# Twenty-five blocks of an adjacency matrix, transposed by a DMA from SBUF to SBUF instead of by TensorE and ScalarE

## The chip, the cores and the metric

The kernel runs on one core of a Trainium2 chip. A core has a matrix engine (TensorE, PE in the profile; its weight loads are PEld), a vector engine (VectorE, DVE), an activation engine (ScalarE, ACT), GpSimd (POOL), and SyncE (SP), which here only issues DMAs. The engines run side by side, each through its own instructions in order, and wait for one another through semaphores. DMAs are moved by 16 DMA engines that all issuers share. The metric is the device time of one execution in microseconds (us), lower being better.

## The reference

A graph of 3,125 nodes with 128 features and 100,000 edges (`src`, `dst`, one of eight types) passes through four graph layers, each followed by a residual and a layer norm. Cut to what matters here:

```
edge_index = stack([src, dst])
x = layernorm(x + L0(x, src, dst))              # three GCN layers: row = src, col = dst
x = layernorm(x + L1(x, edge_index))            # sum of x @ W.T + b over incoming edges
x = layernorm(x + L2(x, edge_index))            # GIN: (1 + eps) x + sum over incoming edges, batchnorms
x = layernorm(x + L3(x, edge_index, type))      # two relational layers: a mean for each of 8 types

# in L0
deg  = segment_sum(1, row)                      # with a self loop for each node
dinv = rsqrt(deg)
h    = segment_sum(dinv[row] * dinv[col] * (h @ W)[col], row) + b
```

L1 and L2 sum over the edges that enter a node, L0 over those that leave it. With the edges as a matrix of counts, L1 and L2 multiply by that matrix and L0 by its transpose. L0 also needs a degree for each node before its first product.

## The kernel before, in words

Nodes are padded to 3,200, that is 25 blocks (`NB`) of 128 (`P`). The kernel has two stretches: one that builds dense matrices of edge counts from the edge list and stores them in HBM, and one that multiplies by them.

**The build** takes the 25 blocks of destination nodes in turn. For block b, `total(b, behind)` counts the edges from each source block s into b:

- VectorE makes one-hot tiles by comparing keys with a ramp (`one_hot`, whose instruction is recorded on L191): `lo` and `hi` for each of two halves u of the block. For the first 15 blocks (`ND`) it also makes `rhq` (L191) and `rlo` (L331), which serve the counts by edge type.
- TensorE multiplies one-hots into the PSUM tile `bld`, which has two buffers. L356 makes the counts of all edges. L339, in `packed_counts`, makes the counts by type, for the first 15 blocks.
- ScalarE evicts `bld`: L359 into `at` (four times in a block), L342 into `rb` (sixteen times in each of the first 15 blocks).
- SP stores `rb` as eight DMAs of 400 KB into `rel` (L369), for the first 15 blocks.

The finished `at` of block b is a tile of 128 destinations by 25 blocks of 128 sources, bf16, 800 KB. `stored(b, at)` is called half-way through the next block's `total`. It adds the self loops on VectorE (L376), stores `at` to `adj_t` (L377), makes the transposed tile `av`, 128 x 3,200 (L378 to L383), stores that to `adj` (L384), and multiplies it by a vector of ones in seven matmuls (L388) that accumulate over the 25 blocks in two PSUM tiles `leave`: the degrees. `at` and `av` have two buffers each.

The transpose in `stored` is 25 TensorE transposes of 128 x 128 (L382), in groups of 13 and 12 into two of the `bld` tiles, each group evicted by one ScalarE copy (L383).

The loop over s also runs the search for the next blocks' edges: small VectorE instructions (L262 to L320) and indirect DMAs issued by GpSimd (L270, L290). These come once for two blocks.

A scheduler places the instructions of each engine in an order of its own, from the program's order and its own expectation of when things are ready. An engine keeps to the order that it was given. So where L388 stands in TensorE's order, and where L384 and L369 stand in SP's, is fixed before the kernel runs.

**After the build** the degrees are copied out of PSUM (L424 to L427), transposed, and turned into `dinv` (L430 to L438). Then the features are scaled and split in two (L662, L583, L584), and the first product begins.

**The products** of the first three layers load `adj` (`load`, L594); L1 and L2 load `adj_t` (L599). ScalarE and VectorE cast the loaded blocks to a wider type (L611, L613) and TensorE multiplies (L628). The relational layer after them reads `rel` (L757), casts (L767), and multiplies (L885). None of these lines is touched.

Of the kernel before, what the change touches and what calls it, by code (L numbers as in the profile page):

```python
# [9 lines left out]
BF = mybir.dt.bfloat16  # L10
# [11 lines left out]
P = 128  # L22
D = 128
N = 3125
NB = 25
# [20 lines left out]
def cols(m0, nb):  # L46
    return slice(m0 * P, (m0 + nb) * P)
# [26 lines left out]
def listed(ctx: ExitStack, tc: tile.TileContext, p: dict, out: bass.AP, bad):  # L74


    nc = tc.nc
# [6 lines left out]
    identb = const.tile([P, P], BF, name="identb")  # L84
# [81 lines left out]
    psum = lists.enter_context(tc.tile_pool(name="f_ps", bufs=1, space=PSUM))  # L166
    with tc.tile_pool(name="f_w", bufs=1) as wp, tc.tile_pool(name="f_bg", bufs=1) as bg:
# [28 lines left out]
        with tc.tile_pool(name="f_t1", bufs=1) as t1:  # L196
# [13 lines left out]
            with tc.high_priority():  # L210
# [5 lines left out]
                t = psum.tile([P, 512], F32, name="mi", tag="mi", bufs=2)  # L216
# [127 lines left out]
            def total(b, behind):  # L344
                at = t1.tile([P, NB, P], BF, name="at", bufs=2)
                rb = t1.tile([P, R * NB, 64], U16, name="rb", bufs=2) if b < ND else None
                for u in range(64 // PU):
                    lo = t1.tile([P, PU // 2, P, 2], BF, name="lo", bufs=2)
                    one_hot(lo, 0, b, u, P)
                    hi = t1.tile([P, PU // 2, 2 * NB, 2], BF, name="hi", bufs=2)  # L350
                    last[0] = one_hot(hi, 1, b, u, 2 * NB, iota50)
                    for v in range(PU // PA):
                        pt = psum.tile([P, PA, 64], F32, name="bld", tag="bld", bufs=2)
                        for k in range(PA):
                            j = v * PA + k
                            nc.tensor.matmul(pt[:, k, : 2 * NB], lo[:, j // 2, :, j % 2],  # L356
                                             hi[:, j // 2, :, j % 2], start=True, stop=True)
                        c0 = 2 * (u * PU + v * PA)
                        nc.scalar.copy(  # L359
                            at[:, :, c0 : c0 + 2 * PA].rearrange("p s (j h) -> p s j h", h=2),  # L360
                            pt[:, :, : 2 * NB].rearrange("p j (h s) -> p s j h", h=2),
                        )
                    if u == 0 and behind is not None:
                        stored(*behind)
                    if b < ND:
                        packed_counts(b, u, lo, rb)
                if b < ND:
                    for r in range(R):
                        nc.sync.dma_start(  # L369
                            rel[r][b].rearrange("p s d -> p (s d)").bitcast(U16),  # L370
                            rb[:, r * NB : (r + 1) * NB, :].rearrange("p s j -> p (s j)"),
                        )
                return b, at

            def stored(b, at):
                nc.vector.tensor_add(at[:, b, :], at[:, b, :], identb)  # L376
                nc.sync.dma_start(adj_t[b], at)  # L377
                av = t1.tile([P, NP], BF, name="av", bufs=2)  # L378
                for m0, nb in ((0, 13), (13, 12)):
                    t = psum.tile([P, 2048], BF, name="bld", tag="bld", bufs=2)  # L380
                    for k in range(nb):
                        nc.tensor.transpose(t[:, cols(k, 1)], at[:, m0 + k, :], identb)  # L382
                    nc.scalar.copy(av[:, cols(m0, nb)], t[:, : nb * P])  # L383
                nc.sync.dma_start(adj[b], av)  # L384
                for i in range(7):
                    w = min(512, NP - 512 * i)
                    q = 32 * (i % 4)
                    nc.tensor.matmul(leave[i // 4][q : q + 32, :w], onesb, av[:, 512 * i : 512 * i + w],  # L388
                                     start=(b == 0), stop=(b == NB - 1), skip_group_check=True)
# [14 lines left out]
            for s in range(SB):  # L404
# [8 lines left out]
                if 2 * s + 1 < NB:  # L413
                    built = total(2 * s + 1, built)
            stored(*built)

            tc.add_manual_dep(words.ins, started[0].ins.name, WAIT, reason="the search comes first")

            dinv = const.tile([P, NB], F32, name="dinv")
            for g in range(2):  # L420
                t = psum.tile([P, 512], F32, name="mi", tag="mi", bufs=2)
# [19 lines left out]
        psum = ctx.enter_context(tc.tile_pool(name="f_bk", bufs=1, space=PSUM, reuse_waits="tile"))  # L441

        def bank(tag):

            return psum.tile([P, 512], F32, name=tag, tag=tag, bufs=4 if tag == "x" else 2)
# [122 lines left out]
        with tc.tile_pool(name="f_nd", bufs=1, reuse_waits="tile") as nd:  # L568
# [85 lines left out]
            t = psum.tile([P, 512], F32, name="mi", tag="mi", bufs=2)  # L654
# [99 lines left out]
    with until_end:  # L754
# [94 lines left out]
        for c, (m0, nb) in enumerate(CH):  # L849
            t = bank(("acc", "x", "x", "x", "x", "mi", "mi")[c])  # L850
            for i in range(nb):
                o = t[:, cols(i, 1)]
                nc.tensor.matmul(o, y2[:, cols(m0 + i, 1)], ident, start=True, stop=False, is_transpose=True)
                nc.tensor.matmul(o, ident, xa[:, m0 + i, :], start=False, stop=True)
            normalise(xa[:, m0 : m0 + nb, :], blocks(t[:, : nb * P]), nb, True)
            split2(xs, m0, nb, x3[:, m0 : m0 + nb, :])
            if c == 1:
                early_cast(2, 1)
            if c > 0:
                stored(*CH[c - 1])  # L860
# [156 lines left out]
        with tc.tile_pool(name="f_hr", bufs=1, reuse_waits="tile") as hp:  # L1017
# [51 lines left out]
            for r in range(R):  # L1069
                nxt = None  # L1070
                for i, (m0, nb) in enumerate(DENSE):
                    inv = load_inv(r, m0, nb)
                    acc = relation(r, m0, nb, hr, work, 2.1, (1, 1, 1, 1, 1))
                    s = hp.tile([P, 512], F32, name="s", bufs=2)
# [628 lines left out]
```

## Time and profile before

| What | Value |
|---|---|
| Median of three runs | 2034.96 us (2032.4 to 2036.95) |
| Profiled execution, its own time | 2027.4 us |
| Its span, first to last instruction | 2025.5 us |
| Mean granted TensorE clock | 0.975 |
| Busy over the span: PE, PEld | 1794.3 us (89%), 1387.0 us (68%) |
| Busy over the span: ACT, DVE, POOL | 1253.0, 1205.1, 859.5 us |
| Build (last L388 begins) | up to 397 us of the span |
| First three layers, L1 and L2 | about 400 to 880 us |
| Relational layer | about 880 us to the end |
| L382, transposes | x625 in the build |
| L383, evictions of them | x50 in the build |
| L388, degree matmuls | x175, 59.6 to 397.0 us |

A busy time is the sum of the recorded durations, and neighbours on ScalarE and VectorE overlap by some 0.1 us in the record, so it is a little above what an engine can't do without. A row of groups reads: line, engine, operation, what it writes and reads, shape, count, then busy us and the mean ns of one, then how long the engine stood idle just before these instructions and what ended that. A row of waits reads: who waited, for whom, us in total, how many times, the longest. A row of windows gives the busy us of each engine in one stretch of the span, the granted TensorE clock, the mean share of time that the 16 DMA engines were busy, and what they moved in GB/s.

### The profile page before, as it was taken

Reading aid. Unit: us, or ns where it says so; the run is one execution under the profiler, and the core shown is the slowest. Engines: PE = TensorE matmul, PEld = TensorE weight load, DVE = VectorE, ACT = ScalarE, POOL = GpSimd, SP = SyncE. Lnnn points to the kernel's source line nnn. Section 1 sums busy time; section 2 is a strip of 40 time slices with the busy share of each in tenths; the row PEclk is TensorE's granted clock in tenths of the full one; section 3 lists DMA queues with packets and bytes.
Section 4 is the critical chain, followed back from the end, with each engine's and each line's share of the span. In section 5 each row is a group of like instructions: output and inputs, shape, how many; then the busy total and the mean of one; then the engine's idle time right before and its main releaser. Section 6 shows DMA issues by size and latency. Waiting matters only on the chain.

```text
span 2025.5 us, 30183 instructions
## 1 busy us (share of the span) xinstructions
PE 1794.3 (89%) x11523; PEld 1387.0 (68%) x11523; DVE 1205.1 (59%) x2055; ACT 1253.0 (62%) x1118; POOL 859.5 (42%) x717
## 2 busy tenths in 40 slices
PE   2677676669999999889999999999999999999897
PEld 1555555458888888667577567758757777777676
DVE  6999998777768863475455345435346444434424
ACT  3999997757888666663233333233338777777774
POOL 5315624120000000027777267706716666666664
PEclk9999998889999999999999999999999999999998
DMA  4766776667888887477677457737659887888773
GB/s 100 277 271 266 291 287 237 247 189 232 255 259 257 251 268 235 140 225 190 177 212 207 148 171 209 188 101 198 184 151 269 243 228 220 235 240 245 196 204 101
DMA packets 398932, 435.67 MB, mean 215 GB/s; under 512 B 27166, under 2 KB 355838, under 8 KB 398776
## 3 DMA queue, kind: packets, MB, share of 16 engines
q1 hardware_dynamic: 346274, 336.92, 53.0%
q0 software_dynamic: 33632, 67.07, 12.9%
q10 hardware_dynamic: 18870, 29.66, 4.9%
q8 instruction: 92, 1.51, 0.3%
q14 instruction: 64, 0.52, 0.1%
HBM read 319.07 MB, written 114.46 MB: 214 GB/s over the span
## 4 chain that ended last, share of the span: by engine, by line
PE 57%; ACT 4%; issue 3%; DVE 3%; another core or an unknown queue 2%; DMA 1%; ACTq 0%; SPq 0%; DVEq 0%
PE acc L885 30%; PE acc L628 8%; PE x L927 8%; PE mi L962 4%; PE mi L975 4%; ACT m L767 3%; PE mi L966 1%; DMA back<-ht_d 1%; PE mi L650 0%; PE x L836 0%; PE mi L740 0%; DVE hilo L790 0%; ACT mf L611 0%; DVE f L1027 0%
## 5 line engine op out<-in xcount | busy, mean ns | idle before, releaser
L885 PE MATMUL acc<-m,hilo 128*128 128x512 f32 (+1 forms) x3200 | 792.3, 393 | 22.8 <-ACT m L767 10.8
L767 ACT CAST m<-m 128x2560 fp32r<-128x2560 uint8 (+1 forms) x225 | 486.8, 2196 | 372.5 <-PE acc L885 148.7
L885 PEld LDWEIGHTS acc<-m,hilo 128*128 128x128 f32 x3200 | 576.5, 190 | 130.3 <-issue 17.6
L919 POOL DMA_INDIRECT gx<-xt_d,gsrc x321 | 366.1, 1140 | 638.5 <-DVE z L1007 413.7
L919 POOL DMA_INDIRECT gx<-ht_d,gsrc x321 | 326.2, 1016 | 200.1 <-issue 72.0
L628 PE MATMUL acc<-mf,halves 128*128 128x512 f32 (+1 forms) x1750 | 383.9, 377 | 11.5 <-DVE mf L613 11.0
L628 PEld LDWEIGHTS acc<-mf,halves 128*128 128x128 f32 x1750 | 320.4, 190 | 60.4 <-DVE mf L613 11.9
L611 ACT CAST mf<-m 128x2560 fp32r<-128x2560 bf16 (+1 forms) x126 | 263.7, 2100 | 67.3 <-PE acc L628 34.8
L927 PE MATMUL x<-oh,gx 128*128 128x192 bf16 (+5 forms) x2208 | 227.1, 239 | 5.5 <-issue 5.2
L927 PEld LDWEIGHTS <-gx 128*128 128x128 bf16 x2208 | 157.0, 97 | 99.2 <-issue 89.6
L767 DVE CAST m<-m 128x2560 fp32r<-128x2560 uint8 (+1 forms) x95 | 158.5, 1670 | 110.6 <-issue 40.3
L909 DVE TENSOR_TENSOR oh<-iota,gkey 128x768 bf16<-128x768 bf16 (+1 forms) x170 | 90.3, 532 | 208.5 <-PE x L927 143.2
L342 ACT CAST rb<-bld 128x800 uint16<-128x800 f32 x240 | 180.0, 847 | 6.5 <-PE bld L339 6.5
L339 PE MATMUL bld<-rhq,rlo 128*128 128x200 bf16 x960 | 124.2, 253 | 49.4 <-ACT rb L342 36.5
L290 POOL DMA_INDIRECT ew<-pk,ptr x26 | 72.7, 2797 | 193.9 <-DVE ptr L285 189.6
L339 PEld LDWEIGHTS <-rlo 128*128 128x128 bf16 x960 | 86.9, 98 | 85.3 <-issue 80.9
L613 DVE CAST mf<-m 128x2560 fp32r<-128x2560 bf16 (+1 forms) x49 | 97.5, 1989 | 70.1 <-PE acc L628 69.9
L191 DVE TENSOR_TENSOR lo<-iota,kT 128x4096 bf16<-128x4096 bf16 x50 | 114.2, 2283 | 11.1 <-PE bld L356 11.1
L191 DVE TENSOR_TENSOR rhq<-iota,kT 128x6400 bf16<-128x6400 bf16 x30 | 104.4, 3480 | 0.0
L975 PE MATMUL mi<-wr,hT 128*128 128x512 f32 x200 | 93.4, 601 | 2.5 <-issue 1.6
L359 ACT CAST at<-bld 128x800 bf16<-128x800 f32 x100 | 79.4, 835 | 20.7 <-PE bld L356 20.6
L270 POOL DMA_INDIRECT g<-in_dst,irow x26 | 76.6, 2947 | 22.9 <-DVE crow L265 9.8
(238 smaller groups left out, 1624.4 us busy)
## 6 DMA issues: line engine op xcount, KB each, us to landing
m<-rel SPq DMA_DIRECT2D x240, 320.0 KB
rel<-rb SPq DMA_DIRECT2D x120, 400.0 KB
m<-adj SPq DMA_DIRECT2D x60, 640.0 KB
m<-adj_t SPq DMA_DIRECT2D x40, 640.0 KB
m<-adj SPq DMA_DIRECT2D x45, 480.0 KB
adj_t<-at SPq DMA_DIRECT2D x25, 800.0 KB
adj<-av SPq DMA_DIRECT2D x25, 800.0 KB
ht_d<-t SPq DMA_DIRECT2D x50, 384.0 KB
```

The source lines that it names most:

```text
L191: return nc.vector.tensor_tensor(o, (iota2 if of is None else of)[:, None, :width, :].to_broadcast([P, PU // 2, width, 2]), k[:, :, None, ...
L339: nc.tensor.matmul(pt[:, k, : R * NB], lo2[:, j // 2, :, j % 2], hq[:, j // 2, :, j % 2], start=True, stop=True)
L342: nc.scalar.copy(rb[:, :, j0 : j0 + 4], pt[:, :, : R * NB].rearrange("p j q -> p q j"))
L611: nc.scalar.copy(v, src)
L613: nc.vector.tensor_copy(v, src)
L628: nc.tensor.matmul(acc[:, :w], x[:, 5 * g + k, :], mf[:, k, :w], start=(g == 0 and k == 0 and i == 0), stop=(more is None and g == 4 and k ...
L767: casts_by[on_act] = nc.scalar.copy(v, src) if on_act else nc.vector.tensor_copy(v, src)
L885: nc.tensor.matmul(acc[:, :w], x[:, 5 * g + k, :], m[:, k, :w], start=(g == 0 and k == 0 and i == 0), stop=(g == 4 and k == 4 and i == 1),)
L909: ins = nc.vector.tensor_tensor(oh[:, : nt // 2], iota2[:, None, : GW * R, :].to_broadcast([P, nt // 2, GW * R, 2]), gkey[:, g, t : t + nt ...
L919: nc.gpsimd.indirect_dma_start(out=gx.rearrange("p i c -> p (i c)"), out_offset=None, in_=table[:], in_offset=bass.IndirectOffsetOnAxis(ap ...
L927: nc.tensor.matmul(acc[a // 512][:, a % 512 : a % 512 + z - a], gx[:, i, :], oh[:, t % 4 // 2, a - c0 : z - c0, t % 2], start=(a // 512 no ...
L975: nc.tensor.matmul(o, hT[:, a, cols(b, 1)], wr[:, a, r : r + 4, :].rearrange("p r c -> p (r c)"), start=(a == 0), stop=(a == 1))
```

## The change

In `stored`, the 25 transposes and the two evictions go. In their place stands one DMA, issued by SP, that reads `at` from SBUF and writes `av` in SBUF transposed: for each source block s, the 128 x 128 block of `at` becomes its transpose in `av`. All that reads `av` (L384, L388) stays as it was, and so does all that makes `at`.

```diff
                 nc.vector.tensor_add(at[:, b, :], at[:, b, :], identb)
                 nc.sync.dma_start(adj_t[b], at)
                 av = t1.tile([P, NP], BF, name="av", bufs=2)
-                for m0, nb in ((0, 13), (13, 12)):
-                    t = psum.tile([P, 2048], BF, name="bld", tag="bld", bufs=2)
-                    for k in range(nb):
-                        nc.tensor.transpose(t[:, cols(k, 1)], at[:, m0 + k, :], identb)
-                    nc.scalar.copy(av[:, cols(m0, nb)], t[:, : nb * P])
+                nc.sync.dma_start(av.rearrange("p (s d) -> p s d", s=NB), at, transpose=True)
                 nc.sync.dma_start(adj[b], av)
```

## The prediction

> **What bounds the kernel now.** The page's busy shares come first and mislead: PE is busy 89% of the span, but the changed lines run only from 55.8 us (first L382) to 397.0 us (last L388), and there TensorE is not the limit. The chain of waits is no help either: its lines (L885, L628, L927) belong to the products. So I read the windows of the build, which has two parts: 66 to 303 us, where blocks also get counts by edge type, and 303 to 394 us, where they don't.
>
> ```profile
> core 0: us, PE busy (x) PEld busy (x) DVE busy (x) ACT busy (x) POOL busy (x), PEclk, DMA share, GB/s
> 66.00:303.00 237.00, 166.44 (x2098) 124.57 (x2096) 231.38 (x264) 230.79 (x292) 90.22 (x25) 1.00 0.71 279
> 303.00:394.00 91.00, 61.23 (x1061) 49.60 (x1060) 75.27 (x119) 71.70 (x78) 28.10 (x17) 0.87 0.61 237
> ```
>
> In the first part VectorE (231.4 of 237) and ScalarE (230.8) are both full, and the DMA engines are busy 71% of the time. Taking work off ScalarE alone can gain only what VectorE then stops waiting for. VectorE's own waits, in the first part and then in the second, say how much that is:
>
> ```profile
> DVE rlo L331 <- PE bld L339: 5.4, 4, 1.8
> DVE at L376 <- ACT at L359: 0.3, 1, 0.3
> ...
> DVE lo L191 <- PE bld L356: 11.1, 7, 4.1
> DVE at L376 <- ACT at L359: 4.0, 1, 4.0
> ```
>
> In 237 us VectorE stands still for 5.7 us. In the next 91 us it waits 11.1 us for TensorE to free `lo`, and 4.0 us at the very end, where it has only the last block's add left. Beside these, what ScalarE and TensorE spend on the transposes (groups of the window 50 to 450 us):
>
> ```profile
> L383 ACT COPY av<-bld 128x1664 bf16<-128x1664 bf16 (+1 forms) x50 | 72.2, 1495 | 9.5 <-PE bld L382 9.5
> ...
> L382 PE MATMUL bld<-identb,at 128*128 128x128 bf16 x625 | 45.1, 235 | 6.3 <-ACT at L359 5.5
> ```
>
> **What goes.** ScalarE loses 50 x 1.495 = 72.2 us, 2.9 us a block in the timeline. TensorE loses 45.1 us, 1.8 us a block. Were ScalarE alone the limit, this would be worth some 70 us. It is not.
>
> First part: SP issues the `rel` stores of successive blocks at 166.04, 184.15, 202.61, ... 312.91 us, a period of 18.36 us. VectorE's own work is 231.4 / 237 x 18.36 = 17.9 us of it. So the most to be gained is the 5.7 us of waits; it comes when TensorE is late behind the transposes and ScalarE's copies. I take 4.5.
>
> Second part: ten blocks in 91 us. The 11.1 us are waits for L356, which itself stands behind L382 and its two `bld` tiles (each must be evicted by L383 before a count can use it). Most should go; not all, since the page of this part still has 3.5 us in which L356 waits for ScalarE's L359. I take 7.5.
>
> **What is added: the DMA's time T.** One DMA a block reads 800 KB (0.82 MB) from SBUF and writes it back turned. The trace has no transposing DMA, and nothing from SBUF to SBUF. Bounds:
>
> - Below: the busiest window of the build (93 to 100 us) moves 358 GB/s at a share of 0.95, so 377 GB/s with all 16 engines busy: 0.82 MB / 377 = 2.2 us. It cannot be below nothing, since no DMA is removed.
> - Nearest row: if the source is read by rows of one 128-column block, these are 256 B pieces, 3,200 of them, 200 to an engine. In the relational layer, whose loads of `rel` have rows of 640 B, the share is 0.72 at 201 GB/s (960 to 1960 us): 17.4 GB/s an engine, 37 ns for 640 B. The 93 to 100 us window, with rows of 3,200 B, gives 23.6 GB/s, 136 ns. A straight line through both gives 22 ns for 256 B, so 200 x 22 = 4.4 us.
> - Above: the Trainium skill, VectorE: DVE Perf Modes, sections "The three transpose paths" and "Rules for kernel authors", speaks against the change: it prices a 128 x 128 bf16 transpose at 1309 ns by DMA and 390 ns by TensorE, and advises TensorE where PSUM will do. Twenty-five DMA transposes in a row would be 32.7 us a block. The trace's row for TensorE is 45.1 / 625 = 72 ns each, back to back, so that single-transpose price is far above the pipelined one there, and I expect the same of a DMA: a lone small one is mostly latency. In this trace the last store, 26.5 KB, is issued at 2020.48 us and the span ends 5.0 us later. By the rule the build would be DMA-bound at (0.71 x 18.36 =) 13.0 + 32.7 = 45.7 us a block. DMA: Bandwidth & Descriptors, section "Latency and other measured facts", has 261 GB/s for a transposing DMA, 3.1 us.
>
> I take T = 4 us, between that and the nearest row.
>
> **Does T fit?** First part: 13.0 + 4 = 17.0 us of DMA in about 18.0. It fits, barely; the edge is T = 5. Second part: 0.61 x 9.1 = 5.6 + 4 = 9.6 us against 9.1; but that share includes the `rel` stores still draining at the start. From 340 to 394 us it is 0.55 on blocks of 8 to 9 us, 4.7 + 4 = 8.7: again just under.
>
> **SP.** Per block it now issues one L377 (0.32 us), eight L369 (6.3 to 7.4 us) and one L384 (0.7 to 1.1): about 8.4 of 18.4 us. The new DMA's issue is one more; even 5 us leave 5 free. L384 now waits on SP for the DMA's end. If the `rel` stores stood behind it they would be some 8 us late, and `rb`, with two buffers, isn't needed again for a block: hidden. `at` stays occupied until the DMA has read it, some 8 us after the add instead of 7; its second buffer covers that in the first part, and in the second it is needed about 9 us after: just hidden, and at most 1 us a block if not.
>
> **The added wait: L388 on TensorE.** Before, L388 begins 8.2 us after the add in a block that I followed (161.1 to 169.35 us). Now `av` lands after 0.5 us of issue, 2.1 us of L377's own 800 KB in the same queue (0.82 MB at 377 GB/s), T = 4, and a completion of some 2 us (an estimate: the last store's 5.0 us less issue and movement): about 8.6 us. Where the order leaves L388 in its old place, TensorE stalls under half a microsecond. Queued behind it are the counts for ScalarE, so a stall passes to ScalarE one for one; ScalarE has the freed 2.9 us a block as cover, and only a stall beyond that lengthens the period.
>
> **The end.** After the last block nothing hides the transpose. Before: add at 393.05, ScalarE begins with the degrees at 397.62, 4.6 us. Now: 8.6 us to `av` and some 1.6 us for seven L388: 10.2 us. That is +5.6; the loads of L594 stand behind L384 on SP and take the same delay. I take +5.5.
>
> **Sum.** -4.5 - 7.5 + 5.5 = -6.5 us. The profiled execution becomes 2027.4 - 6.5 = 2020.9 us, the median 2034.96 - 6.5 = 2028 us. The two before differ by 7.6 us, as one execution from a median of others; I apply the difference. About 0.2%, 4.1 us, is what a measurement of this kernel can tell from no change.
>
> **Rivals.**
>
> 1. *TensorE stalls at L388 (slower).* The scheduler may put L388 where it thinks `av` ready, not where it is. Up to 2.9 us a block it costs nothing; that is the point from which it decides. With L388 at 3 us after the add, and `av` at 8.6, the stall is 5.6: (5.6 - 2.9) x 15 = 40 us, in the second part some 1 us a block, 10, the end 5.5: +55 us, 2090. For it: TensorE's order is fixed, and seven matmuls in it now hang on a shared queue. Against it: before, the matmuls were placed late, and the DMA engines are nearly idle when `at` is done (share 0.42 from 88 to 93 us).
>
> 2. *The DMA engines become the bound (slower).* It decides from T = 5. At T = 8: (13.0 + 8 - 18.4) x 15 = 39, second part (4.7 + 8 - 9) x 10 = 37, end +9.5: +86 us, 2120. For it: the share of 0.71, and the skill's price. Against it: 261 GB/s, and the line through two rows.
>
> 3. *Nothing gained.* VectorE's waits in the build are all replaced by waits of the same size, or the 5.5 us at the end eat the gain: 2035.
>
> 4. *It isn't one DMA of this kind* but a copy of 2-byte pieces; 409,600 of them at 12 ns, where the straight line ends at no bytes, over 16 engines are 307 us a block, 7,700 us in all. The transposing flag makes this unlikely, 2 in 100.
>
> **How the numbers follow.** Forecast (2016 to 2032) 0.45; nothing gained 0.14; rival 1 0.24; rival 2 0.15; rival 4 0.02. The forecast's low end is all 16.8 us of VectorE's waits gone with +5.5 at the end, and some noise: 2034.96 - 11.3 = 2024, less 8 for runs that differ: 2016. The range goes to 2085, most of rival 1 and the mild end of rival 2 (T = 6: 9 + 17 + 7.5 = +34 us). Faster 0.46, same 0.14, slower 0.40.
>
> **What would show it.** Right: no L382, no L383; ScalarE's busy time down by about 72 us and TensorE's by 45; VectorE still over 95% busy in the first part, at a period of 18.0; the DMA share there at about 0.9; L388's waits for the new DMA under 2.9 us a block; the degrees some 10 us after the last add. Wrong: VectorE's idle time growing, with L388 or `at` waiting for a DMA, or a period that follows the DMA share towards 1.

## The result, and the profile after

The changed kernel takes 2042.34 us in the median of 20 runs (2038.07 to 2051.97); the kernel before, beside it, 2032.0 us (20 runs, 2024.1 to 2037.69). The ratio is 1.0056, with a 95% interval of 1.0044 to 1.0068: 0.56% slower, some 11 us. On another chip, in a group of experiments, it was 1.0068 (1.0054 to 1.0081). The profiled execution took 2043 us at a span of 2041.2 us. Line numbers below L383 are four lower in the changed kernel: L388 became L384, L384 became L380, and the new DMA is L379.

First the windows, of the same stretches as before:

```profile
66.00:303.00 237.00, 160.81 (x1799) 114.36 (x1797) 234.47 (x269) 200.85 (x273) 65.47 (x28) 0.89 1.01 323
303.00:394.00 91.00, 40.67 (x710) 30.27 (x709) 69.59 (x111) 33.48 (x46) 16.60 (x13) 0.59 1.06 305
```

In the first part ScalarE has its relief (230.8 to 200.9 us) and VectorE is fuller than before. But the DMA share stands at 1.01, and in the second part at 1.06: the 16 DMA engines have become full. (Records of packets overlap a little there, so the share passes 1.) In the second part everything is less busy than before except the DMA engines. VectorE's waits from 66 to 303 us, and then from 303 to 402 us:

```profile
DVE lo L191 <- PE bld L356: 1.4, 1, 1.4
...
DVE lo L191 <- PE bld L356: 20.0, 7, 8.6
DVE at L376 <- ACT at L359: 4.3, 1, 4.3
```

The 5.7 us of the first part shrank to 1.4; the 11.1 us of the second grew to 20.0. TensorE's and ScalarE's longest waits from 303 to 402 us name what is behind that. Before, the longest wait at the degree matmuls in that part was 1.0 us, for ScalarE's copy; the row of before is first (303 to 394 us), the two of the changed kernel follow:

```profile
PE acc L388 <- ACT av L383: 10.8, 18, 1.0
...
PE acc L384 <- DMA av<-at: 43.7, 11, 9.0
...
ACT at L359 <- DMA av<-at: 41.8, 9, 8.6
```

TensorE stands at the degree matmuls, which need `av`, and ScalarE at the eviction into `at`, whose older block the DMA still reads: two ends of one late transfer. The milestones, read from VectorE's timeline (the add, L376, of a block marks its `at` as complete; `dinv` ends the build), put the loss in its place:

| us | Before | After | Difference of the step |
|---|---|---|---|
| Add of block 0 | 54.84 | 52.69 | -2.2 |
| Add of block 14, the last with `rel` stores | 308.38 | 300.79 | -5.4 |
| Add of block 16 | 328.62 | 330.77 | +9.7 |
| Add of block 24 | 393.05 | 396.12 | +0.9 |
| `dinv` | 401.68 | 412.10 | +7.3 |

The build ends 10.4 us later, which is the difference of the medians. (The two profiled executions differ by 5.3 us more, in the relational layer, which the change doesn't touch.) The changed kernel was 7.6 us ahead when block 14 was done. It lost this and more within two blocks. The timeline of before around the same block, SP's queue alone, and then that of the changed kernel:

```profile
308.62 0.32 SPq L377 DMA_DIRECT2D adj_t<-at  x1
312.91 6.47 SPq L369 DMA_DIRECT2D rel<-rb  x8
```

```profile
300.79 0.22 DVE L376 TENSOR_TENSOR at<-at,identb 128x128 bf16<-128x128 bf16 x1
...
307.22 7.32 SPq L369 DMA_DIRECT2D rel<-rb  x6
...
314.63 0.84 SPq L377 DMA_DIRECT2D adj_t<-at  x1
315.57 7.75 SPq L379 DMA_TRANSPOSE av<-at  x1
...
326.03 1.04 PE L384 MATMUL acc<-av,onesb 128*32 128x512 bf16 x7 [9.02 <-DMA av<-at]
326.09 1.55 ACT L359 CAST at<-bld 128x800 bf16<-128x800 f32 x2 [8.56 <-DMA av<-at]
```

Block 14 is complete at 300.79 us. Its transposing DMA is issued 14.8 us later, because in SP's queue it stands behind the `rel` stores of its block, and `av` lands at 326.0 us, 25 us after the add. The `adj_t` store, too, which before went out 0.24 us after the add and ahead of the `rel` stores, now stands behind them. As long as a block takes 18 us this lag hides. Blocks without `rel` stores take 8 us, and the lag comes due as one stall of 9 us.

### The profile page after: what moved, and what is told of

Its sections match the earlier page's. It is cut to its first block, busy times and chain, and to the rows that moved or that the text cites. A ratio compares the mean times of both kernels' runs of the same rounds, so it can differ in the third digit from the quotient of the medians.

```text
span 2041.2 us, 28891 instructions
## 1 busy us (share of the span) xinstructions
PE 1771.7 (87%) x10898; PEld 1359.2 (67%) x10898; DVE 1205.1 (59%) x2055; ACT 1182.9 (58%) x1068; POOL 810.5 (40%) x717
## 2 busy tenths in 40 slices
DMA packets 479726, 456.06 MB, mean 223 GB/s; under 512 B 107966, under 2 KB 436638, under 8 KB 479576
## 4 chain that ended last, share of the span: by engine, by line
PE 56%; ACT 4%; issue 3%; DVE 3%; another core or an unknown queue 1%; DMA 0%; ACTq 0%; SPq 0%; DVEq 0%
PE acc L881 30%; PE x L923 8%; PE acc L624 7%; PE mi L958 4%; PE mi L971 4%; ACT m L763 2%; PE mi L962 1%; DMA back<-ht_d 0%; PE mi L646 0%; DVE hilo L786 0%; PE x L832 0%; PE mi L736 0%; PE acc L731 0%; ACT mf L607 0%
## 5 line engine op out<-in xcount | busy, mean ns | idle before, releaser
L915 POOL DMA_INDIRECT gx<-xt_d,gsrc x321 | 359.4, 1120 | 650.0 <-DMA inv<-inv_d 414.0
L339 PE MATMUL bld<-rhq,rlo 128*128 128x200 bf16 x960 | 136.8, 274 | 59.1 <-ACT rb L342 35.0
L339 PEld LDWEIGHTS <-rlo 128*128 128x128 bf16 x960 | 96.0, 105 | 101.9 <-issue 77.0
L290 POOL DMA_INDIRECT ew<-pk,ptr x26 | 44.5, 1712 | 233.2 <-DVE ptr L285 228.9
L356 PEld LDWEIGHTS <-lo 128*128 128x128 bf16 x1600 | 58.9, 105 | 39.8 <-issue 22.9
```

The lines of the kernel that those rows point to most:

```text
L339: nc.tensor.matmul(pt[:, k, : R * NB], lo2[:, j // 2, :, j % 2], hq[:, j // 2, :, j % 2], start=True, stop=True)
L915: nc.gpsimd.indirect_dma_start(out=gx.rearrange("p i c -> p (i c)"), out_offset=None, in_=table[:], in_offset=bass.IndirectOffsetOnAxis(ap ...
```

## The experiments

Three theories stood after the trace. **O**: the place in SP's queue. **T**: the time of a transposing DMA on engines that are full. **P**: the place of the degree matmuls in TensorE's order. Each group was run beside the kernel before on one chip; chips differ in absolute time, so ratios are compared. The build hardly differs from chip to chip: the changed kernel's two profiles, of spans 2041.2 and 1981.2 us, have `dinv` at 412.10 and 413.06 us. So its milestones are set side by side.

**The transposing DMA issued early.** The add, the DMA and the `adj_t` store move from `stored` to the point where the block's last eviction is written:

```diff
+                    if u == 1:
+                        av = turned(b, at)      # add, transposing DMA, adj_t store
                     if b < ND:
                         packed_counts(b, u, lo, rb)
```

> The add, the transposing DMA and the adj_t store are issued as soon as the block's at is complete, ahead of the block's eight rel stores in SP's queue and with the transpose ahead of adj_t; in the changed kernel they stand behind the rel stores. Same bytes, same instructions. Theory O (order in SP's queue: the transpose of block b begins 10 to 15 us after its add, and at the switch to blocks without rel stores this lag becomes one stall of 11 us): the stall at the switch goes, and the end is some 2 us shorter, so 11 to 13 us under the changed kernel, that is 0 to 3 us under before. Theory T (the 16 DMA engines are full, share 1.01 to 1.06 in the build): the same bytes take the same time, within 3 us of the changed kernel, 8 us or more over before.

Ratio 1.0013 (0.9999 to 1.0027): about 9 us better than the changed kernel's 1.0056, level with before. The build ended at 403.50 us against 412.10. Its timeline at the same block:

```profile
299.25 0.21 DVE L378 TENSOR_TENSOR at<-at,identb 128x128 bf16<-128x128 bf16 x1
299.49 3.12 SPq L380 DMA_TRANSPOSE av<-at  x1
302.65 0.57 SPq L381 DMA_DIRECT2D adj_t<-at  x1
304.22 6.85 SPq L371 DMA_DIRECT2D rel<-rb  x8
...
311.74 9.37 SPq L380 DMA_TRANSPOSE av<-at  x1
```

The DMA now goes out 0.24 us after the add, and SP is done with it in 3.1 us instead of 7.8. Of the 10.4 us by which the build had become longer, 8.6 are back, so O holds for most of the loss, but not all: it foresaw 11 to 13 us. At the switch itself it gave less. The stall of 9 us at the degree matmuls is gone, but the step from block 14 to 16 still takes 26.2 us, against 30.0 in the changed kernel and 20.2 before. The DMA of block 15, the last line above, has the `rel` stores of block 14 in front of it whichever way and holds SP for 9.4 us, and the share of the first part is still 0.98.

**The degree matmuls a block later, with a third `av`.**

```diff
-                av = t1.tile([P, NP], BF, name="av", bufs=2)
+                av = t1.tile([P, NP], BF, name="av", bufs=3)
 ...
+                if held_av:
+                    degrees(*held_av.pop())       # the seven matmuls of the block before
+                held_av.append((b, av))
```

> The seven degree matmuls of a block are issued one block later on TensorE, with a third av buffer (two small start tiles share the space of others to make room). Theory P (TensorE's order: the degree matmuls stand too early, and everything behind them waits): their wait of 64.7 us shrinks below 10 us and the kernel gains 10 us or more on the changed one, level with before or under it. Theories O and T: the wait moves to the eviction into at, whose buffer the DMA still reads; within 3 us of the changed kernel.

Ratio 1.0135 (1.0112 to 1.0158), and the matmuls' wait was still there: 76.1 us in the build, against 64.7. As a test of P it failed: in the order as built, the degree matmuls of block 22 stand right behind the first half of block 24's counts in both kernels. The scheduler had already put them late, and moving them in the program changed nothing. So P as I had it, matmuls that stand too early by the program, doesn't describe the kernel; the next version gives them a later place after all. Why the third buffer made this one slower than the changed kernel is open. The two start tiles that share space are not it as far as the start shows: the first add came at 52.65 us, as in the changed kernel (52.69).

**A third `at`.**

```diff
-                at = t1.tile([P, NB, P], BF, name="at", bufs=2)
+                at = t1.tile([P, NB, P], BF, name="at", bufs=3)
```

> A third at buffer (two small start tiles share the space of others to make room), all else as changed. If the held at buffer is what stops the build (ScalarE's eviction waits 59.9 us for the transposing DMA), the kernel gains 8 us or more on the changed one. Theory P: TensorE still stands at the degree matmuls, gain under 3 us. Theory O: the lag is the same and the degree matmuls meet it; gain under 3 us.

Ratio 1.0095 (1.0072 to 1.0118): no gain, rather a loss. Yet the blocks did run ahead, as they should with more room: block 16 was done at 320.19 us (330.77 in the changed kernel) and block 24 at 391.62. The time came back at the end, where `dinv` was ready only at 418.14 us:

```profile
391.62 0.22 DVE L376 TENSOR_TENSOR at<-at,identb 128x128 bf16<-128x128 bf16 x1 [6.32 <-ACT at L359]
...
396.75 6.35 SPq L379 DMA_TRANSPOSE av<-at  x1
403.15 0.58 SPq L377 DMA_DIRECT2D adj_t<-at  x1
...
405.34 6.21 SPq L379 DMA_TRANSPOSE av<-at  x1
```

When the last block is complete, two transposes are still to be issued, 8.6 us apart. The stream of DMAs has a pace of its own, and a buffer only moves where the wait is seen. This version also holds the test of P that the last one missed: in its order as built, the degree matmuls of block 14 stand behind the first half of block 17's counts, a block later than in the changed kernel. They still waited 62.3 us in all for `av`. Here a later place didn't help.

**Without the DMA.** `av` is one tile of ones.

```diff
-                av = t1.tile([P, NP], BF, name="av", bufs=2)
-                nc.sync.dma_start(av.rearrange("p (s d) -> p s d", s=NB), at, transpose=True)
```

> The transposing DMA is left out: av is one tile of ones, written once, and is stored and multiplied as before (so the results differ). It shows what taking the transposes off TensorE and ScalarE is worth with nothing in their place: by VectorE's waits of before (5.7, 11.1 and most of the 4.6 us at the end) some 15 to 20 us under before, so 25 to 30 under the changed kernel; the first part still bound by VectorE at about 18 us a block. DMA share in the first part back near 0.71: if it stays at 0.9 or more, the transposes are not what fills the DMA engines.

Ratio 0.989 (0.9868 to 0.9912), 22 us under before:

```profile
66.00:303.00 237.00, 157.34 (x1796) 116.61 (x1791) 237.00 (x270) 206.30 (x281) 66.29 (x27) 0.87 0.76 300
```

VectorE has no idle time left in the record (237.00 of 237), and the DMA share is 0.76. Not all of the 22 us is relief: here `av` waits for nothing, so `dinv` (369.80 us) is ready before the last add (372.41), and the 8.6 us that the kernel before takes from the last add to `dinv` are gone. From the first add to the last it takes 318.9 us against 338.2. So the relief is real, and with 19.3 us larger than the 16.8 us of waits that I had counted; the DMA that buys it costs more than it.

**A plain copy of the same bytes.**

```diff
-                nc.sync.dma_start(av.rearrange("p (s d) -> p s d", s=NB), at, transpose=True)
+                nc.sync.dma_start(av, at.rearrange("p s d -> p (s d)"))
```

> The DMA from at to av stays, same bytes, same place in SP's queue, but copies without transposing (so adj and the degrees differ). Theory T' (what costs is the time that a transposing DMA takes on the 16 engines and on SP, some 5 us a block against 2.2 us for the bytes alone): the build's end comes 10 us or more earlier than in the changed kernel, the whole is under before by 3 to 15 us, and the DMA share in the first part falls to about 0.85. Theory O (the place behind the rel stores, whatever the DMA is): the lag at the switch remains, less than 4 us gained. If bytes alone mattered, nothing would change.

Ratio 1.0003 (0.9993 to 1.0013), with the changed kernel itself beside it on this chip at 1.0068:

> The changed kernel itself, as the yardstick of this group: 0.4 to 0.7% over before by every theory.

The copy is 14 us faster than the transpose. Its windows, the first part and then blocks 16 to 24:

```profile
66.00:303.00 237.00, 163.26 (x1870) 117.20 (x1868) 235.41 (x270) 204.91 (x279) 66.56 (x28) 0.89 0.82 324
323.50:382.00 58.50, 31.43 (x545) 23.27 (x545) 53.55 (x83) 26.11 (x35) 13.93 (x9) 0.53 0.83 338
```

With the copy the DMA engines move 338 GB/s at a share of 0.83 in the blocks without `rel` stores, 7.3 us a block; with the transpose it was 302 GB/s at 1.06, 8.2 us a block:

```profile
330.80:396.10 65.30, 31.49 (x545) 23.71 (x545) 53.88 (x83) 26.12 (x35) 12.33 (x9) 0.55 1.06 302
```

T had foreseen 3 to 15 us under before, and the median is level with it: block 14 to 16 still took 26.5 us, since the copy too stands late in SP's queue (issued 14.5 us after the add of block 14) and TensorE waits 6.3 us for it. Both theories have their part. The copy's profiled execution was the fastest of its 21, and its build ended at 394.86 us, 6.8 us earlier than before; the medians show no such gain, so its milestones flatter it by some us.

**The transpose twice,** the second into a tile that nobody reads. (For room, two small start tiles share the space of others here too.)

```diff
                 nc.sync.dma_start(av.rearrange("p (s d) -> p s d", s=NB), at, transpose=True)
+                av2 = t1.tile([P, NP], BF, name="av2", bufs=1)
+                nc.sync.dma_start(av2.rearrange("p (s d) -> p s d", s=NB), at, transpose=True)
```

> Each transposing DMA is issued twice, the second into a tile that nobody reads. This measures the price of one where the queue is full. Theory T': 25 x 5 = 125 us over the changed kernel, less what slack remains: 90 to 130 us. If a transposing DMA cost only its bytes (2.2 us), 40 to 55 us; if only waiting on the order of SP's queue cost something, under 30 us.

Ratio 1.055 (1.0534 to 1.0567); 96 us over the changed kernel on that chip, 3.8 us for each DMA added.

```profile
132.20:345.10 212.90, 131.01 (x1361) 93.38 (x1360) 173.11 (x195) 151.32 (x205) 51.24 (x23) 0.81 1.09 314
382.70:483.40 100.70, 32.90 (x545) 24.93 (x545) 54.07 (x83) 26.32 (x35) 8.47 (x8) 0.52 1.10 262
```

Here none of the computing engines is full in either part (VectorE, the busiest, 173.1 of 212.9 us and 54.1 of 100.7), so the price can be read twice, as an estimate. Blocks 4 to 14 take 212.9 / 10 = 21.3 us: less the 13.0 us of the stores, 8.3 for two, 4.1 us each. Blocks 16 to 24 take 100.7 / 8 = 12.6 us: less two stores of 0.82 MB at 377 GB/s, 4.35 us, 8.25 for two, 4.1 us each. That is T. But SP was full as well: issues held it for 98.5 of the last 100.7 us. So these 4.1 us alone don't say whether the 16 engines or the queue set the pace. The records of packets give the engines' own part. The page counts 107,966 packets under 512 B in the changed kernel and 27,166 before; nearly all of the difference are 3,200 packets of 256 B for each transposing DMA, 200 to an engine. For the first one, issued at 61.5 us at a share of 0.93, they took 18.4 ns each, 3.7 us in all; in blocks 16 to 24 of the changed kernel 21.5 ns, 4.3 us.

**The transposing DMA only where blocks are long.** Blocks 0 to 13 by DMA, 14 to 24 by TensorE and ScalarE; once issued early, once in the changed kernel's place:

```diff
+                if b < 14:
                     nc.sync.dma_start(av.rearrange("p (s d) -> p s d", s=NB), at, transpose=True)
+                else:
 ...
```

> Blocks 0 to 13 by transposing DMA, issued early as in e_early; blocks 14 to 24 by TensorE and ScalarE as before, so neither the switch nor the end depends on the DMA. By the milestones (block 14 done 7.6 us ahead of before in the changed kernel, 9.1 us in e_early, of which some 2 us lie before the first block) and theory T': 4 to 9 us under before, that is 0.2 to 0.45%. If the gain of the first part is given back wherever TensorE takes over again (its 1.8 us and ScalarE's 2.9 us a block return), within 2 us of before.

> Blocks 0 to 13 by transposing DMA in the changed kernel's order (behind the rel stores), blocks 14 to 24 by TensorE and ScalarE as before. The pair to the early version with the same split (0.9972). If the late place in SP's queue costs most where blocks turn short, the switch still pays part of the lag here, since the av of block 13 lands late: 2 to 6 us over the early version, about level with before. If the place does not matter once the DMA engines have slack at the end, it is within 1.5 us of the early version.

> The kernel of e_early_hyb14 once more, beside the other split on one chip: 0.9972 of before again, 4 to 7 us under it; if that was the chip, within 2 us of before.

Issued early: 0.9972 (0.9960 to 0.9984) and, on another chip, 0.9974 (0.9962 to 0.9985). In the old place: 1.0009 (0.9995 to 1.0023). The first beats both kernels, by 0.27% on before. Its windows:

```profile
66.00:303.00 237.00, 162.93 (x1827) 114.38 (x1824) 231.73 (x265) 201.81 (x274) 117.72 (x27) 0.87 0.98 329
303.00:394.00 91.00, 60.07 (x1023) 48.28 (x1020) 75.04 (x120) 69.35 (x78) 27.42 (x17) 0.83 0.63 245
```

The DMA engines are full only in the first part, and `dinv` is ready at 393.17 us, 8.5 us before the kernel before. In the old place block 16 is done at 330.98 us, the same as in the changed kernel, although blocks 14 to 16 are transposed by TensorE, and the step from block 14 takes 29.7 us against 23.3 with the early issue. The lag of block 13's transpose, which I had expected there, is not what the trace shows: its `av` had landed by 307.4 us and ScalarE waited 1.1 us for it. The `adj_t` store of block 14 had kept the late place behind the `rel` stores, 13.4 us after its add (301.30 us), and ScalarE could write into that buffer again only at 321.5 us:

```profile
314.65 1.20 SPq L377 DMA_DIRECT2D adj_t<-at  x1
...
320.65 0.48 ACT L320 COPY kT<-mi 128x384 bf16<-128x384 bf16 x1 [6.64 <-PE mi L319]
321.53 1.55 ACT L359 CAST at<-bld 128x800 bf16<-128x800 f32 x2 [0.40 <-DMA adj_t<-at]
```

In ScalarE's order a copy of the search stood in front of that write and ended 0.4 us earlier. Which of the two cost the step is not separated.

**Every other block by DMA,** in two versions: over all blocks, and among the first fourteen only.

> Every other block (0, 2, ... 22) by transposing DMA, issued early; the odd ones and the last by TensorE and ScalarE. With a price of 4.1 us for a transposing DMA on a full queue, the DMA engines are asked for 13.0 + 2.1 of 17.6 us a block in the first part and 4.4 + 2.1 of 7.6 in the second: slack in both, and ScalarE keeps half of its relief. If the DMA engines' load is what took the gain away, this is 8 to 14 us under before (ratio 0.993 to 0.996), better than the split at block 14. If the mixing of the two ways costs as much as it saves, within 3 us of before.

> Of blocks 0 to 13 every other one by transposing DMA, issued early; all else by TensorE and ScalarE. Every other block by DMA brought block 14 to 9.0 us ahead of before with the DMA engines at a share of 0.81, and lost it only in the blocks without rel stores; here these are as before. Expected 5 to 9 us under before (0.25 to 0.45%), at least level with all fourteen by DMA. If the gain of the first part is always given back afterwards, within 2 us of before.

Over all blocks: 1.0009 (0.9996 to 1.0021), against an expected 0.993 to 0.996. Block 16 was done at 315.06 us, 13.6 us ahead of before, at a DMA share of 0.81 in the first part. Then blocks 16 to 24 took 76.4 us, against 64.4 before, with the DMA engines not full (0.71 from 330 to 390 us). What took these 12 us is open. From 314 to 392 us TensorE waited for `av` only twice, 3.3 us in all. It waited longest for VectorE's `hi`, 23.2 us in all, and ScalarE stood twice, 8.0 us in all, at an `adj_t` store that SP had issued only after its wait for the `av` of the block before. Among the first fourteen only: 0.9982 (0.9967 to 0.9996), 2.4 us under before, less than expected.

## Why the prediction was wrong

I forecast 0.3% faster, at 2028 us, and it became 0.56% slower. The range held the time; the sign was wrong. Step by step:

- **What goes, first part: right, in part by luck.** -4.5 us were forecast, -5.4 came. The reason held: VectorE was the limit, not ScalarE alone. But the room was larger than I read from the waits: without the DMA, and with the plain copy too, blocks 0 to 14 take 244.4 us against 253.5, 9.1 less. The transposing DMA took 3.7 of these back, with a share of 1.01 where I had forecast 0.9. Two errors nearly cancelled.
- **T: right in size.** I took 4 us, from a line through two rows and a figure of the skill's; the doubled DMA gives 4.1, and the packets 3.7 to 4.3. The reason behind the nearest row, 3,200 pieces of 256 B at 22 ns, is what the record shows, at 18.4 to 21.5 ns. The 261 GB/s of the Trainium skill (DMA: Bandwidth & Descriptors, "Latency and other measured facts") would be 3.1 us; here 0.82 MB in 4.1 us are 200 GB/s, and the measurement decides. The 1309 ns of its page VectorE: DVE Perf Modes ("The three transpose paths") are the price of one block; 25 times that is eight times what one DMA that turns 25 blocks took here.
- **"Does T fit?", second part: wrong, and with it the -7.5 us.** I set 8.7 us of DMA against "blocks of 8 to 9 us". The 9 came from a mean over 91 us that held a slow start: blocks 16 to 24 took 8.05 us each. A gain would have brought them to 7.3, as the copy did, and there 8.5 us of DMA never fit. With a share of 1.06 they took 8.2 us a block: +0.9 us instead of a gain. This was rival 2, which I had let decide only from T = 5; in the short blocks it decided at 4. That the full engines set these 8.2 us is argued from the share and from the copy, and issues held SP for only 47.2 of the 65.3 us. But in SP's queue each transposing DMA there stands behind the `adj` store of the block before, which waits for that block's `av`. So it goes out only after that has landed (block 15's at 332.95 us, the DMA of block 16 at 333.37), and a freer order was not tried.
- **"Landing" and SP: the largest error.** I had the DMA issued half a microsecond after the add, `av` landing at 8.6 us, and `at` "just hidden". I had weighed what the `rel` stores would suffer behind the new wait on SP, but not that the new DMA could be put behind the `rel` stores. It was: issued 14.8 us after the add at block 14, landed at 25 us. Issuing it early took back 8.6 of the build's 10.4 us, so this is shown. Between blocks 14 and 16 the kernel lost 9.7 us, for which my sum had nothing; the early issue took back 3.8 of them, and 6.4 where TensorE transposes from block 14 on. The rest is not split further: the `rel` stores of block 14 are then in front of the DMA of block 15, on engines that are full (1.05 in the early version from 299 to 325 us). Rival 1 named the stall at the degree matmuls, but for another reason and spread evenly. It came in lumps, for the DMA's place and pace: 64.7 us in 17 waits, 43.7 of them between 303 and 402 us, the longest, 9.0 us, at the switch.
- **The end: right in kind, small in size.** +5.5 forecast, +7.3 measured. The DMA of the last block waits on SP behind the store of the block before, and `av` lands 11.2 us after the add, not 8.6.

The sum of the step sizes found is -2.2 - 5.4 + 9.7 + 0.9 + 7.3 = +10.3 us. The first term lies ahead of the first transpose and was nearly absent in the changed kernel's second profile (the add at 54.44 us against 54.84), so it is no gain of the change.

Open: why a third `av` buffer cost more than the changed kernel, and what issuing the add and the `adj_t` store early is worth by itself with TensorE's transposes. For neither was a version run.

## What to carry to other kernels

Work that is moved from an engine to a DMA is not free when the engine was full: set the DMA's time against the period of each kind of block, the shortest first, and against the period that you hope for, not the one that you have. Ask in which place of the issuing queue the scheduler will put it, and what stands in front; a lag that hides behind long blocks is paid at once where blocks become short. Where a stage has both kinds, change only the kind where it fits: here the first fourteen blocks, issued early, for 0.27%.

## What the runs showed of the hardware

- A transposing DMA of 128 x 3,200 bf16 from SBUF to SBUF took 4.1 us on a full queue (an estimate from the doubled DMA), 200 GB/s, and 3.7 us of all 16 DMA engines by the packets of the first one. It moved pieces of 256 B. In blocks of 7.3 us a plain copy of the same bytes left the engines at a share of 0.83 while they moved 338 GB/s.
- It also held the issuing queue far longer than a store. SP's group in the changed kernel has the shortest, the median and the longest issue in ns, against 319 to 1,898 ns for its plain DMAs of that size; with every other block transposed, where the share was 0.81 in the first part, the median was 3.2 us:

```profile
L379 SPq DMA_TRANSPOSE av<-at x25: 4478/5940/8606, 61.5 to 400.5; - x25
```

- The granted TensorE clock was lower where TensorE had less work: in the second part 0.59 in the changed kernel (41 of 91 us busy) against 0.87 before (61 us), and over the build the median degree matmul went from 389 to 582 ns. Without the DMA the clock is as low in both parts (0.87 and 0.54), and that kernel is the fastest, so it is not what decided.
